# Weight rounding in blocks of 2048 columns and feed-forward rows rounded a whole tile at once, in a gated cross-attention kernel

## Chip, core and metric

The kernel runs on one core of a Trainium2 chip. The metric is the device time of one execution in microseconds (us). The engines named below are PE (TensorE), DVE (VectorE), ACT (ScalarE), POOL (GpSimd) and SP (SyncE, which here only issues DMAs). Each engine takes its instructions strictly in the order in which they stand in its queue, as the trace shows.

## What is computed

The reference updates 2048 rows of 512 numbers four times, each time as `x = x + tanh(gain) * layer(layernorm(x))`:

1. each row goes, by its token's class (one of four), through a gated linear unit whose three weights are one batch of the context (512x512);
2. a feed-forward layer with 2048 inner columns, in which activations and weights are rounded to a block float format;
3. an attention with eight heads;
4. a mixture of 64 experts and a shared one, six experts a row.

The change touches the second layer, and the first one in whose shadow the second one's weights are prepared. What the second computes is, shortened:

```python
def _quantize_mx(x, ebits, mfrac, emax_elem, max_norm):   # blocks of 32 along the last axis
    amax = max(abs(xb)); sexp = floor(log2(amax)) - emax_elem; scale = 2 ** sexp
    return _quantize_elem(xb / scale, ebits, mfrac, max_norm) * scale

def _mx_linear(x, w):
    return einsum('bsh,oh->bso', _q_act(x), _q_w(w))

gate = _mx_linear(x, w_gate)         # w_gate, w_up: 2048 x 512
up = _mx_linear(x, w_up)
inter = silu(gate) * up
return _mx_linear(inter, w_down)     # w_down: 512 x 2048
```

## The kernel before

Rows are worked in tiles of 128. There are three large stages in time: the first layer with the weights' rounding beside it, the feed-forward layer, and the attention together with the experts, which makes up more than half of the time and is not touched. In the first two stages the order on PE, ACT, DVE and POOL is written out by hand: the order of the calls in the program is the order in each engine's queue.

**The first stage** (lines 183 to 562). The 2048 rows are sorted by class into 19 tiles. The loop of lines 532 to 559 runs i from -2 to 18, each iteration working on neighbouring tiles: PE turns two tiles (`turned`, L459), turns a part of the rounded weights (`turn_weights`), multiplies by the context (`times_context`, L474, eight fp32 matmuls a call, two calls an iteration). ACT does the copies from PSUM, the silu (L481), the layernorm's application and sums, and DVE does one product a tile (`gated`, L486) and, every fourth tile, a chain of small instructions for the layernorm's factors (`row_factors`).

The rest of DVE's queue is filled with the rounding of the weights. `quantize` (L235) is a generator: it takes a block of 1024 columns by 128 partitions, and rounds it in ten DVE instructions and one ACT copy (L251, `mx_wide`, the block scales spread out to all columns). After each step it yields a number of microseconds, a guess of the step's time written in the code. `some_weights(us)` takes steps until their guesses have used up `us`. There are 24 blocks: 8 of each of the three weights. A rounded block goes to the list `rounded`; `turn_weights` takes one from it, and its eight PE transposes and two ACT copies bring it into `wgT`, `wuT` or `wdT` (L204, L205, L219, L221). What is left after the loop is done in lines 560 to 562. `fetch_weights` issues the DMA of a block on SP's queue: one block is fetched first of all, three after the context's second load.

**The feed-forward stage** (lines 565 to 747). For each of 16 tiles: `gate_up(j, c)` makes 512 gate columns and 512 up columns, each in a PSUM buffer of its own (`gu`, four buffers, four matmuls each, L642); `silu` (ACT, L652) reads the gate half; `times_up` (DVE, L656) multiplies by the up half and so frees that buffer. `block_scales` takes the maxima of blocks of 32 (L587), two small steps (L588, L590) and has ACT spread the scales (`mx_wide`, L592); `block_round` divides (L603), cuts off (L609) and multiplies by `mx_wide` (L610). `turned_hidden` and `turned_rows` transpose the rounded numbers on PE (L622) and copy them out on ACT (L623, into `iT` and `hT`); `down` makes the output (L662), `add_rows` scales it (L667) and adds it to the rows in memory with a DMA of POOL. The inner rows (2048 columns, called "a") are rounded in two halves of 1024 columns; the input rows (512 columns, called "h") are rounded one tile ahead. `load` (L578) reads a tile back from memory on SP's queue; the tiles of this stage lie in memory that the first stage has given up.

## Time and profile before

| | us |
|---|---|
| median of three runs (1250.85 to 1265.53) | 1256.01 |
| the profiled execution | 1259.73 |
| its span, first instruction to last | 1257.5 |

The profile comes from that one execution. The stages in it, with the busy time of three engines in us:

| stretch of the span, us | what | DVE | PE | ACT |
|---|---|---|---|---|
| 0 to 38.9 | sorting, context turned, first rows arrive | 23.32 | 13.60 | 12.70 |
| 38.9 to 62.2 | the first layer starts | 21.57 | 13.10 | 18.29 |
| 62.2 to 230.0 | its loop | 159.66 | 153.58 | 105.85 |
| 230.0 to 251.0 | the last tile and the last weights | 18.95 | 8.49 | 6.34 |
| 251.0 to 283.0 | the feed-forward starts | 15.75 | 9.00 | 18.71 |
| 283.0 to 491.3 | 14 tiles of it | 194.38 | 174.97 | 134.82 |
| 491.3 to 514.8 | its last two | 16.25 | 18.02 | 10.98 |
| 514.8 to 1257.5 | attention and experts | 349.07 | 627.66 | 257.74 |

Busy time leaves out the gaps of some tens of ns from one instruction to the next. In a timeline below, each line is: start in us, duration in us, engine, line of the code, operation, output tile and input tiles, shape, how many instructions were merged, and in brackets how long the engine had been idle before it and what ended that.

### The profile page before, as it was taken

The numbers are of one execution on the slowest core, as the hardware profiler recorded it, in microseconds if no ns is written. First come the engines' busy times: TensorE is split into PE (matmuls) and PEld (weight loads), VectorE is DVE, ScalarE is ACT, GpSimd is POOL, SyncE is SP. The second block draws the span as 40 slices with busy tenths as digits, with TensorE's granted clock in tenths as the row PEclk, the third lists the DMA queues.
The fourth block names the chain that finished last, engine by engine and source line by source line (L and its number), as shares of the span: only waits on it lengthen the run. The fifth ranks groups of instructions, "written<-read, shape, count | busy, mean of one in ns | idle before, by whom it ended". The sixth has DMA issues, their size and how long they took to land. (4 is left out here: it accounts for less than half of the span.)

```text
span 1257.5 us, 14877 instructions
## 1 busy us (share of the span) xinstructions
PE 1018.4 (81%) x4603; PEld 516.6 (41%) x4603; DVE 799.0 (64%) x1993; ACT 565.4 (45%) x1128; POOL 381.8 (30%) x526
## 2 busy tenths in 40 slices
PE   4489999528878788367999998982699999999994
PEld 4244454213434344133444444441355555544441
DVE  7799999949999999425888788774122222222221
ACT  3666765356767565245666666650111111211120
POOL 3023222100000000001354454455354444444424
PEclk9699999769999999687999999996799999999997
DMA  9834434221211111591112121119699999999977
GB/s 336 303 84 111 116 76 100 26 93 33 36 19 23 17 18 17 156 279 51 62 52 65 58 62 43 37 49 232 195 277 281 275 271 273 267 275 279 279 195 137
DMA packets 75806, 174.76 MB, mean 139 GB/s; under 512 B 13024, under 2 KB 14064, under 8 KB 75664
## 3 DMA queue, kind: packets, MB, share of 16 engines
q1 hardware_dynamic: 51696, 128.04, 34.3%
q0 software_dynamic: 23200, 45.16, 18.4%
q8 instruction: 38, 0.62, 0.2%
q10 hardware_dynamic: 832, 0.62, 0.2%
q14 instruction: 40, 0.33, 0.1%
HBM read 133.76 MB, written 44.20 MB: 142 GB/s over the span
## 5 line engine op out<-in xcount | busy, mean ns | idle before, releaser
L1188 PE MATMUL gu_ps<-e_gu,gT 128*96 128x384 f32 x512 | 178.1, 491 | 0.1
L1192 DVE SCALAR_TENSOR_TENSOR a<-s,xg,gu_ps 96x192 f32<-96x192 f32 x64 | 35.1, 548 | 153.4 <-ACT s L1190 153.4
L1211 PE MATMUL e_y<-e_dn,eaT 96*96 96x512 f32 x256 | 120.5, 592 | 0.1
L123 POOL DMA_INDIRECT taken<-token_no,to_i x96 | 97.1, 1011 | 48.8 <-issue 24.1
L848 ACT ACTIVATE p<-at_s,low 128x512 f32<-128x512 f32 x128 | 87.5, 695 | 50.5 <-DVE low L839 50.5
L834 PE MATMUL at_s<-c_tile,q 64*128 64x512 f32 x256 | 76.6, 679 | 37.1 <-ACT p L848 21.7
L1188 PEld LDWEIGHTS gu_ps<-e_gu,gT 128*96 128x96 f32 x512 | 79.2, 165 | 62.5 <-issue 62.2
L839 DVE TENSOR_REDUCE low<-at_s 128x2 f32<-128x1024 f32 x64 | 77.8, 1217 | 36.7 <-PE at_s L834 36.3
L1213 ACT COPY e_o<-e_y 96x512 f32<-96x512 f32 x64 | 37.3, 582 | 132.9 <-PE e_y L1211 61.3
L1180 DVE COPY gT<-g_ps 128x384 f32<-128x384 f32 x64 | 35.7, 558 | 94.4 <-PE g_ps L1178 94.4
L668 POOL DMA_DIRECT2D x_rows<-y_sb x16 | 13.7, 857 | 259.7 <-ACT y_sb L667 204.9
L859 ACT COPY pT<-p_ps 128x512 f32<-128x512 f32 x128 | 70.9, 597 | 41.3 <-PE p_ps L858 41.0
L491 POOL DMA_INDIRECT x_rows<-y_sb,to_row x19 | 37.1, 1955 | 152.9 <-ACT y_sb L490 152.9
L1214 POOL DMA_INDIRECT out_dram<-e_o,idx x34 | 48.8, 1435 | 114.4 <-ACT e_o L1213 52.7
L858 PEld LDWEIGHTS p_ps<-ident,p 128*128 128x128 f32 x512 | 56.7, 144 | 59.5 <-issue 24.2
L858 PE MATMUL p_ps<-ident,p 128*128 128x128 f32 x512 | 75.2, 287 | 6.6 <-ACT hT L936 6.4
L1165 POOL DMA_INDIRECT xg<-h_rows,idx x64 | 60.1, 938 | 64.4 <-DVE a L1192 29.2
L642 PEld LDWEIGHTS <-hT 128*128 128x128 bf16 x512 | 49.9, 101 | 70.0 <-issue 12.8
L474 PE MATMUL l_mm<-cT,sT 128*128 x152 | 75.9, 646 | 0.3 <-ACT sT L461 0.3
L642 PE MATMUL gu<-wgT,hT 128*128 128x512 bf16 x256 | 70.8, 402 | 6.4 <-ACT hT L623 6.4
L1190 ACT ACTIVATE s<-gu_ps 96x192 f32<-96x192 f32 x64 | 20.9, 327 | 119.1 <-PE gu_ps L1188 119.1
L474 PE MATMUL l_mm<-cT,hT 128*128 x152 | 71.5, 614 | 1.7 <-ACT hT L461 1.7
(239 smaller groups left out, 2019.7 us busy)
## 6 DMA issues: line engine op xcount, KB each, us to landing
e_gu<-in_L_ffn_w_gate_dram SPq DMA_DIRECT2D x64, 384.0 KB, 15.7
e_gu<-in_L_ffn_w_up_dram SPq DMA_DIRECT2D x64, 384.0 KB, 16.1
e_dn<-in_L_ffn_w_down_dram SPq DMA_DIRECT2D x64, 384.0 KB, 15.6
w_src<-in_L_ffn_w_gate_dram SPq DMA_DIRECT2D x8, 512.0 KB, 5.2
c_sb<-in_ctx_dram SPq DMA_DIRECT2D x4, 1024.0 KB, 8.3
w_src<-in_L_ffn_w_up_dram SPq DMA_DIRECT2D x8, 512.0 KB, 4.9
more_rows<-zeros SPq DMA_DIRECT2D x16, 256.0 KB, 8.1
w_src<-in_L_ffn_w_down_dram SPq DMA_DIRECT2D x8, 512.0 KB, 4.5
```

The lines of the kernel that those rows point to most:

```text
L123: ins = nc.gpsimd.indirect_dma_start(out=table[:, :], out_offset=bass.IndirectOffsetOnAxis(ap=to, axis=0), in_=what, in_offset=None)
L474: nc.tensor.matmul(ps.unsqueeze(1), aT[:, k, :], cT[:, bass.ds(at + k, 1), :], start=k == 0, stop=k == KC - 1)
L642: nc.tensor.matmul(ps, hT[:, k, :], wT[:, k, bass.ts(c, 512)], start=k == 0, stop=k == KC - 1)
L834: nc.tensor.matmul(s[:, h, :], t["q"][rows, bass.ts(i, P)], t["c"][rows, :], start=True, stop=True)
L839: nc.vector.tensor_reduce(low, tiles[j]["s", i], AX.X, ALU.max, negate=True)
L848: nc.scalar.activation(p[:, h, :], s[:, h, :], AF.Exp, bias=low[:, h : h + 1], accum_out=t["sums"][:, i, h : h + 1])
L858: nc.tensor.transpose(ps[:, k, :], p[:, h, bass.ts(k, P)], ident)
L859: nc.scalar.copy(tiles[j]["pT"][h][:, :, bass.ts(i, P)], ps)
L1165: nc.gpsimd.indirect_dma_start(out=g[:, :], out_offset=None, in_=h_rows[:, :], in_offset=bass.IndirectOffsetOnAxis(ap=idx[:, e : e + 1], a ...
L1188: nc.tensor.matmul(ps, gT[:, k, :], gu[:, :, k, :], start=k == 0, stop=k == KC - 1)
L1211: nc.tensor.matmul(y, aT[:, c, :], dn[:, c, :], start=c == 0, stop=c == 1)
L1214: nc.gpsimd.indirect_dma_start(out=tables[e % 2 if e < E - LAST else 0][:, :], out_offset=bass.IndirectOffsetOnAxis(ap=idx[:, e : e + 1], ...
```

## The change

The weights are rounded in 12 blocks of 2048 columns. The buffers of the sources go from 4 of 1024 columns to 3 of 2048, those of `w_q` from 3 to 2, those of `mx_wide` from 2 to 1; one block is fetched first and two more later. A rounded block is turned in two parts, each of eight transposes and now one ACT copy of 1024 columns. The guesses that `quantize` yields are new, and `some_weights` now carries over to its next call what a step took too much or too little. After the loop two parts are turned each time round.

In the feed-forward stage the inner rows are multiplied, rounded and turned a whole tile of 2048 columns at once; the order of the loop is new, and the input rows are rounded two tiles ahead.

```diff
-            src = qp.tile([P, 2, D], F32, name="w_src", bufs=4)
+            src = qp.tile([P, 4, D], F32, name="w_src", bufs=3)
...
-            def turn(q):
+            def turn(q, part):
...
-                    nc.scalar.copy(wT[:, k : k + 2, bass.ts(rb, 2 * P)], ps.rearrange("p i j q -> p i (j q)"))
+                nc.scalar.copy(wT[:, k : k + 2, bass.ts(rb, 4 * P)], ps.rearrange("p i j q -> p i (j q)"))
...
         def quantize():
-            n = 2 * D
+            n = 4 * D
...
-                yield 1.21
+                yield 2.3
...
-                wide = qp.tile([P, n], BF16, name="mx_wide")
+                wide = qp.tile([P, n], BF16, name="mx_wide", bufs=1)
...
-                rounded.append((turn, q))
-                yield 0.69
+                rounded.extend([(turn, q, 0), (turn, q, 1)])
+                yield 1.25
...
+        credit, ended = [0.0], []
         def some_weights(us):
-            while us > 0:
+            credit[0] += us
+            while credit[0] > 0:
                 took = next(weights, None)
...
-                us -= took
+                credit[0] -= took
...
                 if b == 1:
-                    fetch_weights(3)
+                    fetch_weights(2)
...
-        while rounded or sources:
-            some_weights(8.0)
+        while rounded or not ended:
+            some_weights(16.0)
+            turn_weights()
             turn_weights()
...
+        times_up(0, 0)
+        gate_up(0, 2)
+        silu(0, 2)
+        times_up(0, 1)
+        gate_up(0, 3)
+        silu(0, 3)
         for j in range(4, 6):
             sums_of(j)
+        block_scales(1, "h", D)
+        block_round(1, "h", D)
+        turned_rows(1)
```

The guesses of the nine steps go from 1.21, 0.36, 1.22, 0.69, 0.69, 1.22, 1.22, 0.5, 0.69 to 2.3, 0.4, 2.3, 1.25, 1.25, 2.3, 2.3, 0.7, 1.25. The loop over the tiles of the feed-forward, before and after:

```python
# before
if j:
    turned_hidden(j - 1, 1)
times_up(j, 0)
times_up(j, 1)
gate_up(j, 2)
silu(j, 2)
block_scales(j, ("a", 0), half_n)
block_round(j, ("a", 0), half_n)
gate_up(j, 3)
silu(j, 3)
if j:
    down(j - 1)
if j + 8 < NT:
    load(j + 8)
sums_of(j + 6)
if j + 2 < NT:
    normal(j + 2)
if more:
    block_scales(j + 1, "h", D)
    block_round(j + 1, "h", D)
if j:
    add_rows(j - 1)
if more:
    turned_rows(j + 1)
turned_hidden(j, 0)
if more:
    gate_up(j + 1, 0)
    silu(j + 1, 0)
times_up(j, 2)
times_up(j, 3)
block_scales(j, ("a", 1), half_n)
if more:
    gate_up(j + 1, 1)
    silu(j + 1, 1)
block_round(j, ("a", 1), half_n)
factors_from(j + 3)
```

```python
# after
times_up(j, 2)
times_up(j, 3)
block_scales(j, "a", FI)
if more:
    gate_up(j + 1, 0)
    silu(j + 1, 0)
    gate_up(j + 1, 1)
    silu(j + 1, 1)
if j:
    down(j - 1)
block_round(j, "a", FI)
if j + 8 < NT:
    load(j + 8)
if j + 2 < NT:
    normal(j + 2)
sums_of(j + 6)
if j:
    add_rows(j - 1)
if more:
    times_up(j + 1, 0)
    times_up(j + 1, 1)
    gate_up(j + 1, 2)
    silu(j + 1, 2)
    gate_up(j + 1, 3)
    silu(j + 1, 3)
turned_hidden(j)
if j + 2 < NT:
    block_scales(j + 2, "h", D)
    block_round(j + 2, "h", D)
    turned_rows(j + 2)
factors_from(j + 3)
```

`turned_hidden(j)` now makes 16 transposes into two PSUM buffers and two ACT copies of 1024 columns into `iT`.

More of the change, by code (lines that the diff above doesn't have):

```diff
@@ L193, in rows_of @@
         def rows_of(w, wT, rb):
-            src = qp.tile([P, 2, D], F32, name="w_src", bufs=4)
-            nc.sync.dma_start(src, w[bass.ts(rb, 2 * P), :].rearrange("(j p) d -> p j d", p=P))
-            def turn(q):
-                q = q.rearrange("p (j d) -> p j d", j=2)
-                for k in range(0, KC, 2):
-                    ps = ps_t.tile([P, 2, 2, P], BF16, name="w_ps", tag="t")
-                    for i in range(2):
-                        for j in range(2):
-                            nc.tensor.transpose(ps[:, i, j, :], q[:, j, bass.ts(k + i, P)], ident_bf)
-                    nc.scalar.copy(wT[:, k : k + 2, bass.ts(rb, 2 * P)], ps.rearrange("p i j q -> p i (j q)"))
@@ L207, in rows_of @@
-            return src.rearrange("p j d -> p (j d)"), turn
-        def half_row_of_down(ob, half):
-            n = FI // 2
-            src = qp.tile([P, n], F32, name="w_src", bufs=4)
-            nc.sync.dma_start(src, w_down[bass.ts(ob, P), bass.ts(half, n)])
-            def turn(q):
-                for c in range(0, n // P, 4):
-                    ps = ps_t.tile([P, 4, P], BF16, name="w_ps", tag="t")
-                    for i in range(4):
-                        nc.tensor.transpose(ps[:, i, :], q[:, bass.ts(c + i, P)], ident_bf)
-                    at = half * (n // P) + c
-                    nc.scalar.copy(wdT[:, at : at + 4, bass.ts(ob, P)], ps)
+            src = qp.tile([P, 4, D], F32, name="w_src", bufs=3)
@@ new lines, in rows_of @@
+            nc.sync.dma_start(src, w[bass.ts(rb, 4 * P), :].rearrange("(j p) d -> p j d", p=P))
+            def turn(q, part):
+                q = q.rearrange("p (j d) -> p j d", j=4)
+                ps = ps_t.tile([P, 2, 4, P], BF16, name="w_ps", tag="t")
+                k = 2 * part
+                for i in range(2):
+                    for j in range(4):
+                        nc.tensor.transpose(ps[:, i, j, :], q[:, j, bass.ts(k + i, P)], ident_bf)
+                nc.scalar.copy(wT[:, k : k + 2, bass.ts(rb, 4 * P)], ps.rearrange("p i j q -> p i (j q)"))
@@ new lines, in rows_of, with row_of_down, turn @@
+            return src.rearrange("p j d -> p (j d)"), turn
+        def row_of_down(ob):
+            src = qp.tile([P, FI], F32, name="w_src", bufs=3)
+            nc.sync.dma_start(src, w_down[bass.ts(ob, P), :])
+            def turn(q, part):
+                ps = ps_t.tile([P, 8, P], BF16, name="w_ps", tag="t")
+                for i in range(8):
+                    nc.tensor.transpose(ps[:, i, :], q[:, bass.ts(8 * part + i, P)], ident_bf)
+                nc.scalar.copy(wdT[:, bass.ts(part, 8), bass.ts(ob, P)], ps)
@@ L223, in half_row_of_down @@
             return src, turn
-        blocks = [(rows_of, (w, wT, rb)) for rb in range(FI // (2 * P)) for w, wT in ((w_gate, wgT), (w_up, wuT))]
-        blocks += [(half_row_of_down, (ob, half)) for ob in range(KC) for half in range(2)]
+        blocks = [(rows_of, (w, wT, rb)) for rb in range(FI // (4 * P)) for w, wT in ((w_gate, wgT), (w_up, wuT))]
+        blocks += [(row_of_down, (ob,)) for ob in range(KC)]
         sources, rounded = deque(), deque()
@@ L249, in quantize @@
                 nc.vector.tensor_scalar(inv.bitcast(I32), top.bitcast(I32), -1.0, float(254 << 23), ALU.mult, ALU.add)
-                wide = qp.tile([P, n], BF16, name="mx_wide")
+                wide = qp.tile([P, n], BF16, name="mx_wide", bufs=1)
                 nc.scalar.copy(wide.rearrange("p (k b) -> p k b", b=BLK), top.unsqueeze(2).to_broadcast([P, nb, BLK]))
-                yield 0.36
+                yield 0.4
                 nc.vector.tensor_tensor(s3, s3, inv.unsqueeze(2).to_broadcast([P, nb, BLK]), ALU.mult)
-                yield 1.22
+                yield 2.3
                 e = qp.tile([P, n], F32, name="mx_e", bufs=1)
                 nc.vector.tensor_scalar(e.bitcast(I32), src.bitcast(I32), EXP_MASK, None, ALU.bitwise_and)
-                yield 0.69
+                yield 1.25
                 nc.vector.tensor_scalar(e, e, 0.25, None, ALU.max)
-                yield 0.69
+                yield 1.25
                 nc.vector.scalar_tensor_tensor(src, e, magic, src, ALU.mult, ALU.add)
-                yield 1.22
-                q = qp.tile([P, n], BF16, name="w_q", bufs=3)
+                yield 2.3
+                q = qp.tile([P, n], BF16, name="w_q")
                 nc.vector.scalar_tensor_tensor(q, e, -magic, src, ALU.mult, ALU.add)
                 fetch_weights(1)
-                yield 1.22
+                yield 2.3
                 nc.vector.tensor_scalar(q, q, 1.5, -1.5, ALU.min, ALU.max)
-                yield 0.5
+                yield 0.7
                 nc.vector.tensor_mul(q, q, wide)
-                rounded.append((turn, q))
-                yield 0.69
+                rounded.extend([(turn, q, 0), (turn, q, 1)])
+                yield 1.25
         left = deque(blocks)
         weights = quantize()
+        credit, ended = [0.0], []
         def some_weights(us):
-            while us > 0:
+            credit[0] += us
+            while credit[0] > 0:
                 took = next(weights, None)
                 if took is None:
+                    ended.append(True)
                     return
-                us -= took
+                credit[0] -= took
         def turn_weights():
             if rounded:
-                turn, q = rounded.popleft()
-                turn(q)
+                turn, q, part = rounded.popleft()
+                turn(q, part)
         def turn_context(b):
@@ L628, in turned_rows, with turned_hidden @@
             stages[j]["hT"] = hT
-        def turned_hidden(j, half):
-            if half == 0:
-                stages[j]["iT"] = fp.tile([P, FI // P, P], BF16, name="iT")
-            n = FI // 2
-            turned(j, ("a", half), n, ps_a, stages[j]["iT"], half * (n // P))
+        def turned_hidden(j):
+            iT = fp.tile([P, FI // P, P], BF16, name="iT")
+            q = stages[j].pop(("q", "a"))
+            n = FI // P // 2
+            for half in range(2):
+                ps = ps_a.tile([P, n, P], BF16, name="q_ps", tag="q_ps")
+                for c in range(n):
+                    nc.tensor.transpose(ps[:, c, :], q[:, bass.ts(half * n + c, P)], ident_bf)
+                nc.scalar.copy(iT[:, bass.ts(half, n), :], ps)
+            stages[j]["iT"] = iT
         def gate_up(j, c):
@@ L646, in silu @@
         def silu(j, c):
-            half = c // 2
-            if c % 2 == 0:
-                stages[j]["a", half] = fp.tile([P, FI // 2], F32, name="inter")
-            part = stages[j]["a", half][:, bass.ts(c % 2, 512)]
+            if c == 0:
+                stages[j]["a"] = fp.tile([P, FI], F32, name="inter")
+            part = stages[j]["a"][:, bass.ts(c, 512)]
             nc.scalar.activation(part, stages[j]["gu", c][0], AF.Silu, scale=16.0)
         def times_up(j, c):
-            part = stages[j]["a", c // 2][:, bass.ts(c % 2, 512)]
+            part = stages[j]["a"][:, bass.ts(c, 512)]
             nc.vector.tensor_mul(part, part, stages[j].pop(("gu", c))[1])
@@ L685, in factors_from @@
                     stages[t]["stats"] = s
-        half_n = FI // 2
         for j in range(8):
@@ L703, in flamingo_kernel @@
         silu(0, 1)
+        times_up(0, 0)
[4 more added lines that the diff above has]
+        silu(0, 3)
         for j in range(4, 6):
             sums_of(j)
+        block_scales(1, "h", D)
+        block_round(1, "h", D)
+        turned_rows(1)
         for j in range(NT):
+            times_up(j, 2)
+            times_up(j, 3)
+            block_scales(j, "a", FI)
             more = j + 1 < NT
-            if j:
-                turned_hidden(j - 1, 1)
-            times_up(j, 0)
-            times_up(j, 1)
-            gate_up(j, 2)
-            silu(j, 2)
-            block_scales(j, ("a", 0), half_n)
-            block_round(j, ("a", 0), half_n)
-            gate_up(j, 3)
-            silu(j, 3)
+            if more:
+                gate_up(j + 1, 0)
+                silu(j + 1, 0)
+                gate_up(j + 1, 1)
+                silu(j + 1, 1)
             if j:
                 down(j - 1)
+            block_round(j, "a", FI)
             if j + 8 < NT:
                 load(j + 8)
-            sums_of(j + 6)
             if j + 2 < NT:
                 normal(j + 2)
-            if more:
-                block_scales(j + 1, "h", D)
-                block_round(j + 1, "h", D)
+            sums_of(j + 6)
             if j:
@@ L731, in flamingo_kernel @@
             if more:
-                turned_rows(j + 1)
-            turned_hidden(j, 0)
-            if more:
-                gate_up(j + 1, 0)
-                silu(j + 1, 0)
-            times_up(j, 2)
-            times_up(j, 3)
-            block_scales(j, ("a", 1), half_n)
-            if more:
-                gate_up(j + 1, 1)
-                silu(j + 1, 1)
-            block_round(j, ("a", 1), half_n)
+                times_up(j + 1, 0)
[5 more added lines that the diff above has]
+            turned_hidden(j)
+            if j + 2 < NT:
+                block_scales(j + 2, "h", D)
+                block_round(j + 2, "h", D)
+                turned_rows(j + 2)
             factors_from(j + 3)
-        turned_hidden(NT - 1, 1)
         down(NT - 1)
```

## The prediction, made before the changed kernel ran

> **What bounds the kernel now.** I read the page's forty slices first, then busy time by stage, then the timelines of DVE, ACT and PE over two tiles of the feed-forward, then those of the first stage and SP's waits.

> ```profile
> DVE  7799999949999999425888788774122222222221
> ```

> Slices are 31.4 us. DVE is full in slices 3 to 7 (the first layer with the weights' rounding) and 9 to 15 (the feed-forward). These are the two stretches that the change touches. DVE's timeline around one half of the inner rows:

> ```profile
> 400.50 0.68 DVE L587 TENSOR_REDUCE mx_top<-h 128x16 f32<-128x512 f32 x1
> ...
> 402.36 0.43 DVE L609 TENSOR_SCALAR mx_c<-mx_q 128x512 bf16<-128x512 fp8e4 x1
> 402.89 0.43 DVE L610 TENSOR_TENSOR mx_c<-mx_c,mx_wide 128x512 bf16<-128x512 bf16 x1
> 403.23 1.28 DVE L656 TENSOR_TENSOR inter<-inter,gu 128x512 f32<-128x512 f32 x2
> 404.55 1.22 DVE L587 TENSOR_REDUCE mx_top<-inter 128x32 f32<-128x1024 f32 x1
> ...
> 406.24 1.23 DVE L603 TENSOR_TENSOR mx_q<-inter,mx_inv 128x1024 fp8e4<-128x1024 f32 x1
> 407.49 0.69 DVE L609 TENSOR_SCALAR mx_c<-mx_q 128x1024 bf16<-128x1024 fp8e4 x1
> 408.29 0.69 DVE L610 TENSOR_TENSOR mx_c<-mx_c,mx_wide 128x1024 bf16<-128x1024 bf16 x1
> 408.90 1.28 DVE L656 TENSOR_TENSOR inter<-inter,gu 128x512 f32<-128x512 f32 x2
> ```

> No line has an idle bracket: a half takes 408.90 - 403.23 = 5.67, the input rows 403.23 - 400.50 = 2.73, a tile 2 x 5.67 + 2.73 = 14.07. The reduction costs 0.71 start to start at 512 columns and 1.25 at 1024, so some 0.17 of each instruction is fixed. ACT and PE in the same tile:

> ```profile
> 401.42 0.62 ACT L592 CAST mx_wide<-mx_top 128x512 bf16<-128x512 f32 x1
> ...
> 403.81 0.59 ACT L623 COPY hT<-q_ps 128x512 bf16<-128x512 bf16 x1 [0.58 <-PE q_ps L622]
> 404.29 1.02 ACT L623 COPY iT<-q_ps 128x1024 bf16<-128x1024 bf16 x1
> ```

> The scales of the input rows are spread (401.42) before any `iT` copy: the copy stands early in ACT's queue, and DVE finds it done. That is what the change turns round.

> ```profile
> SPq L578 <- DMA x_rows<-y_sb,to_row: 29.8, 1, 29.8
> SPq L578 <- DVE w_q L268: 3.4, 1, 3.4
> SPq L578 <- PE w_ps L219: 1.1, 1, 1.1
> ```

> SP's waits show what the feed-forward's first load (issued at 251.07) waited for in turn: the first layer's last rows in memory, then the last block's rounding, last its transposes.

> **First stage, change by change.** Prices of 2048 columns are extended from the rows of 512 and 1024. A block of 1024 takes 8.06 (from 233.68 to 241.74). At 2048: reduction 2.33, two small steps 0.5, division 2.29, mask and maximum 1.27 each, the two roundings 2.33 each, cut 0.80, product 1.15: 14.27. In all 24 x 8.06 = 193.4 becomes 12 x 14.27 = 171.2.

> Where that falls follows from the guesses. Before, each of the 21 iterations gets exactly one block (4.17 and 3.63 of guesses), two go ahead of the loop, one is left. After, the guesses sum to 12 x 14.05 = 168.6, and the calls hand out 14.5 + 42 x 3.6 = 165.7: only the last cut and product are left. From the first rows' arrival (38.9) to the last `gated` (ends 230.0) DVE's weight steps are 161.8 before and 147.0 after. I take 14 off, since the trace runs 1 under its own rows here.

> Behind that last `gated`, the load comes at +21.0. After, 11.9 of DVE steps remain, then 16 transposes, eight in 0.83 at the slow pace of 508.44: 13.6, so -7.

> Against it: PE needs 8.25 a tile in unbroken stretches (87.83 to 96.08), 18 tiles 148.5, while DVE's own sum for these falls to 9.3 blocks (132.7), 18 products (10.8) and four chains of factors (13.2): 156.7. Eight us of play over 18 tiles is little, and from iteration 9 the copy L251 falls in the second call of its iteration, where ACT, waiting for a reduction of 2.3, holds up the copy of `sT` queued behind it, and PE's product with it. Between 0 and +8, I take +4, the middle: no row shows it. And 3 MB of weights instead of 2 go ahead of the first rows' gathers in a stretch where the DMA is 91% busy at 313 GB/s: 0 to +3.3, I take +2, as half of the megabyte stands ahead of the context. Sum: -14 - 7 + 4 + 2 = **-15** (-22 to -9). The two-part turns with one copy of 1.01 for two that take 1.07 cost nothing: ACT has 105.9 of 167.8 busy in that loop.

> **Feed-forward, DVE alone.** A block of 2048: reduction 2.33, small steps 0.5, division 2.29, cut 1.34, product 1.15, together 7.61; with four L656 (2.64) 10.25 instead of 11.34. DVE alone would need 10.25 + 2.73 = 12.98 a tile, 1.09 less.

> **Feed-forward, the new wait.** The last instruction of the input rows (L610) needs `mx_wide`, and in the new order ACT's copy for it is queued behind both `iT` copies of the tile. Put tile j's L656 for column 2 at 0. The block ends at 8.93, the next tile's L656 for column 0 at 9.61, for column 1 at 10.25, and DVE reaches the input rows' L610 at 12.64. On the other side: of the four `gu` buffers, that L656 frees the one that `gate_up(j+1, 2)` wants for its up half. PE goes on 0.06 later (as at 427.00), does three groups of four at 0.866 (up 2, gate 3, up 3): 12.27. Then `turned_hidden`: its first copy starts 0.66 after the transposes (409.04 to 409.70): 12.93; the two copies take 0.91 each start to start: 14.75; then `mx_wide` 0.60: 15.35. So L610 runs at 15.38, **2.74 late**, and the next tile starts at 15.72. Queued behind L610 on DVE is the next tile's L656, and PE's `turned_rows` waits for it. ACT is no bound on the way: its spread of 2048 (about 1.9, from 0.62 and 1.04) is done at 5.9, y at 10.0.

> PE restarts at 1.22 (L610 to the first gate matmul was 1.56) and has, up to gate 2, five groups and 16 matmuls of `down` (3.47): it ends at 9.02, 0.65 before its wait. But it has been idle for 2.5 us and done 0.25 of transposes. What such a gap does:

> ```profile
> 77.90 0.92 PE L204 MATMUL w_ps<-ident_bf,w_q 128*128 128x128 bf16 x8 [2.57 <-DVE w_q L268]
> 78.61 5.08 PE L474 MATMUL l_mm<-cT,sT 128*128 x8
> 83.52 3.60 PE L474 MATMUL l_mm<-cT,hT 128*128 x8
> ...
> 115.90 1.04 PE L204 MATMUL w_ps<-ident_bf,w_q 128*128 128x128 bf16 x8 [2.53 <-DVE w_q L268]
> 116.72 4.80 PE L474 MATMUL l_mm<-cT,sT 128*128 x8
> ```

> The eight matmuls behind the gap take 1.2 to 1.5 longer than the eight after them; at 153.76 and 191.18 gaps of 2.50 do the same. In the feed-forward, restarts cost 0.93 (284.37 to 288.76 for four groups, 3.46 when undisturbed) to 1.69 (435.87 to 441.02). Less the 0.65 of play: 0.3 to 1.0 a tile, so 16.0 to 16.8; I take 16.4. [...]

> Sum over 14 tiles, from L656 of column 2 in tile 0 to the same in tile 14: before 491.30 - 282.95 = 208.3. After, eleven at 16.4, three at 15.7 behind which DVE's factors (3.3, as at 422.97) give PE the time to recover, and those factors: 180.4 + 47.2 + 9.9 = 237.5, **+29.2** (all warm 230.0, +21.7; all at 16.8 241.9, +33.6). Start: `mx_wide` of tile 1 follows silu 3 and four sums on ACT, so that L656 starts at 282.4 instead of 282.95, -0.5. End: the last tile's L656 of column 3 waits for PE until 12.5, its block ends at 20.8, and the last output copy comes 5.76 later as before plus a second `iT` copy of 0.91: 27.5 instead of 514.06 - 491.30 = 22.8, +4.7 (4.2 to 5.2). Feed-forward **+33.4** (25.4 to 38.3). `load`, `normal` and the sums move by a few us inside the tile and hold up nobody: the rows are loaded eight tiles ahead. The later stages (742.7) are unchanged.

> **Sum.** +33.4 - 15 = +18.4. The profiled execution (1259.7, span 1257.5) would become 1278; it lies 3.7 over the median, and on the median it is 1256.0 + 18.4 = 1274, 1259 to 1285 with all bounds.

> **Rivals.** *The wait doesn't come (faster).* If `mx_wide` were done when DVE reaches L610, each tile takes 12.98: 14 x 12.98 + 9.9 - 208.3 = -16.7, with ends -12.5, with the first stage -27.5: 1228. It hangs on one number, the 2.74: below 1.96 the change breaks even, below 1.06 it is faster by over 1%. For it: `h` itself is ready early. Against: ACT ran in program order wherever I looked, and the 2.74 doesn't contain any extended price of DVE; it is PE's and ACT's steps behind one L656 (5.8) less 3.0 of DVE. *PE stays warm:* +25.9 - 15 = +10.9, 1267. *The first stage doesn't pay:* PE's 8.25 and ACT's held copies eat 10 of the 14, so -5: 1284.

> **Chances.** Forecast 0.50, warm 0.20, first stage unpaid 0.14, no wait 0.16. One per cent, about what can be told from no change, is 12.6 us: 1243.4 to 1268.6. Slower: most of the forecast, all of the unpaid first stage: 0.58. Same: most of the warm case and the forecast's low end: 0.27. Faster: 0.15. The range leaves out the case without the wait and little else: 1250 to 1290.

> **What would show it.** L610 of the input rows idle for 2.7 to 3.5 before it, ended by ACT `mx_wide`; tiles of 16 to 17; PE's four-groups above 1.03 behind each such gap; the first load at 233 to 240. Wrong would be: DVE without idle time in the feed-forward, or a first load later than 245.

## The result, and the profile after

| | before | after |
|---|---|---|
| median, four runs each | 1255.89 | 1302.11 (1299.60 to 1303.33) |
| profiled execution / its span | 1259.73 / 1257.5 | 1302.19 / 1300.4 |
| first load of the feed-forward issued | 251.07 | 263.45 |
| from there to the last `y_sb` | 262.99 | 294.97 |
| from there to the end | 743.4 | 742.0 |

The ratio is 1.036 (1.029 to 1.042): slower, and above the range of 1250 to 1290. The feed-forward lost 32.0 (forecast 33.4). The first stage was to gain 15 and lost 12.4; nearly the whole miss is there. Line numbers of the changed kernel are a few higher: `gated` is L487, `turned` L460 and L462, `times_context` L475, the rounding's last step L612, `times_up` L663.

The forty slices of the changed kernel, DVE's row, now 32.5 us each:

```profile
DVE  7788778737877787731688888786222222222231
```

Neither stretch that was full of 9s before is full now: DVE waits in both. Its timeline over one tile of the feed-forward:

```profile
413.91 1.28 DVE L663 TENSOR_TENSOR inter<-inter,gu 128x512 f32<-128x512 f32 x2
415.23 2.29 DVE L589 TENSOR_REDUCE mx_top<-inter 128x64 f32<-128x2048 f32 x1
...
425.85 0.43 DVE L611 TENSOR_SCALAR mx_c<-mx_q 128x512 bf16<-128x512 fp8e4 x1
430.31 0.43 DVE L612 TENSOR_TENSOR mx_c<-mx_c,mx_wide 128x512 bf16<-128x512 bf16 x1 [4.03 <-ACT mx_wide L594]
430.65 1.28 DVE L663 TENSOR_TENSOR inter<-inter,gu 128x512 f32<-128x512 f32 x2
```

A tile takes 430.65 - 413.91 = 16.74, of which 4.03 is the wait for `mx_wide`; the reduction of 2048 columns takes 2.29, as it was extended (2.33). ACT's timeline in the same tile shows what `mx_wide` is queued behind:

```profile
427.83 1.93 ACT L641 COPY iT<-q_ps 128x1024 bf16<-128x1024 bf16 x2 [0.71 <-PE q_ps L640]
429.64 0.63 ACT L594 CAST mx_wide<-mx_top 128x512 bf16<-128x512 f32 x1
```

And PE's timeline shows what the wait does to its clock (four matmuls take 1.03 when undisturbed):

```profile
430.79 0.40 PE L624 MATMUL q_ps<-ident_bf,mx_c 128*128 128x128 bf16 x4 [2.55 <-DVE mx_c L612]
431.86 1.44 PE L650 MATMUL gu<-wgT,hT 128*128 128x512 bf16 x4 [0.68 <-ACT hT L625]
433.10 1.91 PE L650 MATMUL gu<-wuT,hT 128*128 128x512 bf16 x4
434.81 1.51 PE L650 MATMUL gu<-wgT,hT 128*128 128x512 bf16 x4
436.15 1.03 PE L650 MATMUL gu<-wuT,hT 128*128 128x512 bf16 x4
```

The granted clock of the profile is 0.50 of full speed from 432.35 to 435.76, and 1.00 before and after.

A wait, a gap and slow groups of this kind the prediction had described. What it hadn't is in the first stage. There, DVE's product `gated` (L486 before, now L487) had no idle time ahead of it before (0.0); now it has 25.3 in all, 25.1 of it ended by ACT's silu (L482). In these two lines, the first from before, stand the busy time of all 19, the mean ns of one, and the idle time ahead of them:

```profile
L486 DVE TENSOR_TENSOR s<-s,l_mm 128x512 f32<-128x512 f32 x19 | 12.9, 680 | 0.0
```

```profile
L487 DVE TENSOR_TENSOR s<-s,l_mm 128x512 f32<-128x512 f32 x19 | 13.0, 685 | 25.3 <-ACT s L482 25.1
```

One such wait, followed back through three timelines of the changed kernel: DVE, ACT, PE.

```profile
93.62 2.29 DVE L260 SCALAR_TENSOR_TENSOR w_q<-mx_e,w_src 128x2048 bf16<-128x2048 f32 x1
99.24 0.69 DVE L487 TENSOR_TENSOR s<-s,l_mm 128x512 f32<-128x512 f32 x1 [3.33 <-ACT s L482]
```

```profile
93.91 1.01 ACT L205 COPY wgT<-w_ps 128x1024 bf16<-128x1024 bf16 x1 [3.99 <-PE w_ps L204]
94.81 0.81 ACT L170 ACTIVATE h<-xs,ln_shift,ln_y 128x512 f32<-128x512 f32 x1
...
97.66 0.56 ACT L462 COPY sT<-l_ps 128x512 f32<-128x512 f32 x1
...
98.60 0.61 ACT L482 ACTIVATE s<-l_mm 128x512 f32<-128x512 f32 x1
```

```profile
93.26 0.61 PE L204 MATMUL w_ps<-ident_bf,w_q 128*128 128x128 bf16 x8
...
95.68 0.66 PE L460 MATMUL l_ps<-ident,h 128*128 128x128 f32 x4 [1.37 <-ACT h L170]
98.28 5.17 PE L475 MATMUL l_mm<-cT,sT 128*128 x8 [1.94 <-ACT sT L462]
103.28 3.60 PE L475 MATMUL l_mm<-cT,hT 128*128 x8
```

Read from the bottom. The loop has a second `turn_weights` for the case that more than one part waits in `rounded`; it stands behind both products of the iteration. Before, one block of one part came each iteration, and it ran once, in the first iteration, since two blocks were ready ahead of the loop (PE's eight transposes at 52.65, behind a product). Now a block adds two parts in every second iteration, and it runs each time:

```python
            if waiting > 1:
                turn_weights()
            if i + 3 < NS:
                normal(i + 3)
```

Its eight transposes (93.26) come only when PE is through its products, so ACT stood idle for 3.99 before the copy of the turned part (93.91), although the factors that the `normal` behind it reads had been ready since 68.4. Behind this copy were queued `normal` (94.81), the output rows, the sums, and then `sT` (97.66). PE waited 1.37 and 1.94 for these, its next eight matmuls took 5.17 instead of 3.65 after the gap, and the silu and DVE's product came late. Such a pair of iterations takes 20 to 23 us (from the transposes of L460 at 85.01 to 106.71, 126.95, 149.86), against 2 x 9.3 before. The DVE work did fall as computed (the weights' steps are busy 167.1 in all, 187.1 before), and DVE waited instead.

SP's waits of the changed kernel, for the feed-forward's first load, have one line left of the three:

```profile
SPq L580 <- DMA x_rows<-y_sb,to_row: 60.1, 1, 60.1
```

PE's last transposes of weights end at 259.0; the load, issued at 263.45, waits last for the last tile's rows, whose `y_sb` is at 257.39.

### The profile page after: what moved, and what is told of

Read it like the earlier page. It is cut to its first block, busy times and chain, and to the rows that moved or that the text cites. A ratio compares the mean times of both kernels' runs of the same rounds, so it can differ in the third digit from the quotient of the medians.

```text
span 1300.4 us, 14538 instructions
## 1 busy us (share of the span) xinstructions
PE 1036.2 (80%) x4603; PEld 521.6 (40%) x4603; DVE 765.3 (59%) x1777; ACT 558.6 (43%) x1076; POOL 386.6 (30%) x526
## 4 chain that ended last, share of the span: by engine, by line
PE 41%; DMA 14%; DVE 11%; ACT 7%; issue 3%; POOL 1%; SPq 0%; DVEq 0%; POOLq 0%; ACTq 0%
PE gu L650 9%; DMA out_dram<-e_o,idx 8%; PE gu_ps L1197 8%; PE e_y L1220 5%; PE first_ps L952 3%; PE y L669 3%; PE at_o L900 3%; DVE low L848 3%; PE at_s L843 2%; PE sh_y L1274 2%; ACT iT L641 2%; PE p_ps L867 2%; ACT p L857 1%; DMA e_gu<-in_L_ffn_w_gate_dram 1%; DMA e_dn<-in_L_ffn_w_down_dram 1%
## 5 line engine op out<-in xcount | busy, mean ns | idle before, releaser
L857 ACT ACTIVATE p<-at_s,low 128x512 f32<-128x512 f32 x128 | 87.5, 695 | 53.8 <-DVE low L848 51.9
L475 PE MATMUL l_mm<-cT,sT 128*128 x152 | 83.5, 700 | 16.4 <-ACT sT L462 16.4
L650 PE MATMUL gu<-wgT,hT 128*128 128x512 bf16 x256 | 77.2, 431 | 21.9 <-ACT hT L625 13.9
L650 PEld LDWEIGHTS <-hT 128*128 128x128 bf16 x512 | 53.9, 108 | 98.8 <-issue 38.5
L650 PE MATMUL gu<-wuT,hT 128*128 128x512 bf16 x256 | 75.8, 425 | 0.0
```

Of the source, the lines that this page charges most:

```text
L475: nc.tensor.matmul(ps.unsqueeze(1), aT[:, k, :], cT[:, bass.ds(at + k, 1), :], start=k == 0, stop=k == KC - 1)
L650: nc.tensor.matmul(ps, hT[:, k, :], wT[:, k, bass.ts(c, 512)], start=k == 0, stop=k == KC - 1)
L857: nc.scalar.activation(p[:, h, :], s[:, h, :], AF.Exp, bias=low[:, h : h + 1], accum_out=t["sums"][:, i, h : h + 1])
```

## The experiments

Theory: the first stage's loss is the second turn's ACT copy, queued behind PE's products and ahead of ACT's work for the next tile; the feed-forward's loss is `mx_wide` behind the `iT` copies, and the clock that PE loses in the gap. Rivals: the first stage loses through the DMA of larger blocks or through PE's load, or PE's place for the transposes is at fault rather than ACT's; in the feed-forward, two copies ahead of `mx_wide` aren't enough, or the clock has nothing to do with it. All eight kernels ran in two groups; the kernel before had a median of 1250.51 beside the first (the two halves, the early second turn, the input rows first) and of 1259.10 beside the second. So ratios are compared, and the stages of the profiles:

| | ratio to before | first load | to last `y_sb` | rest | L487 / L612 wait |
|---|---|---|---|---|---|
| before | 1 | 251.07 | 262.99 | 743.4 | 0.0 / 3.4 |
| after | 1.036 | 263.45 | 294.97 | 742.0 | 25.3 / 54.3 |
| feed-forward alone | 1.0296 | 251.55 | 295.22 | 742.5 | 0.8 / 54.0 |
| weights alone | 1.0147 | 259.55 | 265.10 | 735.0 | 22.4 / 3.2 |
| second turn ahead of the products | 1.0166 | 231.80 | 295.54 | 742.1 | 3.3 / 54.5 |
| second turn's copy behind the sums | 1.0101 | 233.69 | 294.74 | 740.9 | 2.5 / 53.8 |
| input rows ahead of turned inner rows | 0.9997 | 264.20 | 249.63 | 733.4 | 26.2 / 8.5 |
| only their scales ahead | 1.0043 | 260.10 | 257.52 | 744.9 | 22.6 / 13.2 |
| spare transposes in the gap | 1.0193 | 262.80 | 279.28 | 739.2 | 24.8 / 38.3 |
| both orders mended | 0.9742 | 232.49 | 249.45 | 741.9 | 3.4 / 7.2 |

"First load" is when the feed-forward's first load is issued; the L612 column is what DVE waits there for ACT's `mx_wide`. The rest, which no kernel touches, lies between 733.4 and 744.9: hence the stages, not the totals, carry the readings.

**The two halves of the change.** The first kernel has the feed-forward of the change behind the first stage of before, the second the first stage of the change ahead of the feed-forward of before.

> First stage of before, feed-forward of the change. In the changed kernel the feed-forward, from its first load to its last output copy, takes 295.0 us (263.45 to 558.42) against 263.0 before (251.07 to 514.06), and the first load comes 12.4 later. If the two halves of the change add up: first load at 251, feed-forward 295, time 1256 + 32 = 1288. Rival, that the feed-forward is slow because of what the first stage leaves behind (the layout of the memory, a colder PE): well under 1288, near 1256.

> First stage of the change, feed-forward of before. If the halves add up: first load at 263.5, feed-forward 263.0, time 1256 + 12.4 = 1268. Rival as in the run beside it: 1256 or 1300.

Measured: 1288.23, ratio 1.0296 (1.0250 to 1.0341), and 1265.85, 1.0147 (1.0112 to 1.0181). In the profiles the feed-forward costs 32.2 with the old first stage too, and the first stage 8.5 with the old feed-forward, with 22.4 of L487's waits. So each half loses without the other. Whether the first stage's loss is the same in both (8.5 here, 12.4 in the whole change) can't be told: in the five kernels with this first stage the first load lies between 259.55 and 264.20. That 1288 was met is in part luck: the first kernel took 37.7 longer than the kernel before in its own group, and 32.7 longer by the stages.

**The second turn directly behind the first, ahead of both products.** The work is the same; only the place in the queues of PE and ACT changes.

```diff
             if waiting:
                 turn_weights()
+            if waiting > 1:
+                turn_weights()
...
-            if waiting > 1:
-                turn_weights()
             if i + 3 < NS:
```

> The second part's turn moves up behind the first one's, ahead of both products. Theory: the 27 us between the forecast for the first stage (first load 15 earlier) and what came (12.4 later) are ACT's queue, held by the second part's copy until PE has done two products. Then the first load comes at 236 to 243, DVE's waits for the silu go from 24 us to under 8, and the time is 1275 to 1282. Rival, that blocks of 2048 are at fault themselves (steps of 2.3 us, an ACT spread of 1.9, later fetches): first load within 4 of 263, time within 5 of 1302.

Measured: 1270.59, ratio 1.0166 (1.0143 to 1.0190). The first load comes at 231.80, 31.7 before the changed kernel's and 19.3 before the old one's; load and time both come below what was expected. In PE's timeline of this kernel the 16 transposes stand together, and the products follow each other:

```profile
80.36 1.06 PE L204 MATMUL w_ps<-ident_bf,w_q 128*128 128x128 bf16 x16
81.26 3.65 PE L475 MATMUL l_mm<-cT,sT 128*128 x8
...
89.45 3.70 PE L475 MATMUL l_mm<-cT,sT 128*128 x8 [0.24 <-ACT sT L462]
```

On ACT the two copies run as soon as `sT` and `hT` are out, with no idle time in front:

```profile
81.09 1.95 ACT L205 COPY wgT<-w_ps 128x1024 bf16<-128x1024 bf16 x2
```

The larger blocks, their DMA and all transposes are still in this kernel: they are not what the first stage lost by.

**PE's place or ACT's.** The second turn stays behind both products on PE; its transposes come as late as in the changed kernel. On ACT its copy moves behind `normal`, the output rows and the sums.

```diff
-            if waiting > 1:
-                turn_weights()
             if i + 3 < NS:
                 normal(i + 3)
...
             sums_of(i + 7)
+            if waiting > 1:
+                turn_weights()
```

> The second part's turn stays behind both products on PE, but moves on ACT behind the layernorm's application, the output copy and the sums. PE's own order is as in the changed kernel. Theory: it is ACT's order that costs, so nearly all of the first stage's loss comes back: first load at 231 to 238, time 1270 to 1278. Rival, that it is the place of the transposes on PE: first load at 263, time 1302.

Measured: 1273.44, ratio 1.0101 (1.0057 to 1.0145), first load at 233.69. ACT's timeline of this kernel:

```profile
142.12 1.01 ACT L205 COPY wuT<-w_ps 128x1024 bf16<-128x1024 bf16 x1 [1.15 <-PE w_ps L204]
143.03 0.59 ACT L462 COPY sT<-l_ps 128x512 f32<-128x512 f32 x1
```

ACT still waits for the transposes, but 1.15 instead of 3.99, because the work that was queued behind the copy is now done while PE multiplies. PE's wait for `sT` is 11.0 in all, against 16.4 in the changed kernel and 7.3 with the early turn. 29.8 of the 31.7 us come from ACT's order alone.

**The input rows ahead of the turned inner rows.** In the feed-forward's loop, the three calls for the input rows move ahead of `turned_hidden(j)`, so ACT spreads their scales before it copies `iT`.

```diff
-            turned_hidden(j)
             if j + 2 < NT:
                 block_scales(j + 2, "h", D)
                 block_round(j + 2, "h", D)
                 turned_rows(j + 2)
+            turned_hidden(j)
```

> In the feed-forward, scales, rounding and turn of the input rows go ahead of the turn of the inner rows; the first stage is the change's. Theory: without ACT's copies ahead of the spread scales, DVE never waits and a tile takes 12.98; 14 tiles take 191.6 with the factors instead of 235.0, so the time is 1302 - 43 = 1259, the feed-forward 252. Rival, that rounding a whole tile of 2048 at once makes the chain too long wherever the scales stand: tiles stay above 15, time above 1290.

Measured: 1249.73, ratio 0.9997 (0.9969 to 1.0024), with the first stage's loss still in it. DVE's timeline of this kernel over a tile:

```profile
413.83 1.28 DVE L663 TENSOR_TENSOR inter<-inter,gu 128x512 f32<-128x512 f32 x2
...
417.42 0.42 DVE L612 TENSOR_TENSOR mx_c<-mx_c,mx_wide 128x512 bf16<-128x512 bf16 x1
...
426.65 1.28 DVE L663 TENSOR_TENSOR inter<-inter,gu 128x512 f32<-128x512 f32 x2
```

The tile takes 12.82 and L612 doesn't wait; the prediction had 12.98 for DVE alone. The feed-forward takes 249.63, 13.4 less than before the change (the prediction's rival without the wait had 12.5) and 45.3 less than after it; against the first stage's loss of 13.1 in this profile that makes the ratio of 1. So the blocks of 2048 columns do pay what DVE's prices say, if the order lets them.

**Only the scales ahead.** Here `mx_wide` is ahead of `iT` on ACT, but the rounded input rows are still turned behind the inner rows on PE, and `hT` copied behind `iT`.

```diff
+            if j + 2 < NT:
+                block_scales(j + 2, "h", D)
             turned_hidden(j)
             if j + 2 < NT:
-                block_scales(j + 2, "h", D)
```

> In the feed-forward only the scales of the input rows (and with them ACT's spread) go ahead of the turn of the inner rows; their rounding's turn, and the copy of hT, stay behind it. Theory: DVE's wait for the spread goes, since it hung on that one copy's place; what is left is the loop of PE and ACT, from the first gate matmul over twelve groups, down, 16 transposes, two copies and the copy of hT back to it, 13.5 a tile against DVE's 12.8: time some 10 above the 1250 of the run with the whole turn moved, 1255 to 1265. Rival, that the turn and the copy of hT behind the inner rows were the harm and not the spread: tiles above 15, time above 1285.

Measured: 1262.27, ratio 1.0043 (1.0012 to 1.0075); the feed-forward takes 257.52. DVE's wait falls to 0.78 in a tile (13.2 in all), but now PE waits for `hT`, as its timeline shows:

```profile
432.99 0.81 PE L650 MATMUL gu<-wgT,hT 128*128 128x512 bf16 x3 [2.00 <-ACT hT L625]
433.64 1.03 PE L650 MATMUL gu<-wuT,hT 128*128 128x512 bf16 x4
```

Of the 45.3 us that the full order gains, the place of `mx_wide` alone gives 37.5; the other 7.9 is `hT` behind `iT`. Note that the groups after this gap of 2.00 are at full pace. But in the same kernel the shorter gaps of 1.42 and 0.90 around the four transposes at 446.71 are followed by groups of 1.87 and 1.91.

**Spare transposes in PE's gap.** The order of the change is kept, with its wait for `mx_wide`. Ahead of each `turned_rows` PE does 40 transposes of the unit matrix, whose result the real ones overwrite.

```diff
+            for c in range(spare):
+                nc.tensor.transpose(ps[:, c % 4, :], ident_bf, ident_bf)
...
-            turned(j, "h", D, ps_h, hT, 0)
+            turned(j, "h", D, ps_h, hT, 0, spare=40 if j > 1 else 0)
```

> The changed kernel with 40 idle transposes of the unit matrix ahead of each turn of the input rows, into the buffer that the turn then overwrites, so that PE is not idle while it waits. Theory: the tiles that take 16.7 do so since PE's clock falls in the gap of 2.5 us and the next groups of four take 1.4 to 1.9 instead of 1.03; kept busy, these tiles take 15.7 as forecast without the clock, the wait of DVE goes from 4.0 to 2.8, 11 tiles x 1.0 = 11 off, 1291. Rival, that the gap has nothing to do with the slow groups: no change, 1302, groups still slow.

Measured: 1283.97, ratio 1.0193 (1.0156 to 1.0229). PE's timeline of this kernel:

```profile
434.35 2.40 PE L624 MATMUL q_ps<-ident_bf 128*128 128x128 bf16 x40
437.06 0.40 PE L626 MATMUL q_ps<-ident_bf,mx_c 128*128 128x128 bf16 x4 [0.32 <-DVE mx_c L612]
438.37 0.81 PE L652 MATMUL gu<-wgT,hT 128*128 128x512 bf16 x3 [0.91 <-ACT hT L627]
439.01 1.03 PE L652 MATMUL gu<-wuT,hT 128*128 128x512 bf16 x4
```

And DVE's:

```profile
421.87 1.28 DVE L665 TENSOR_TENSOR inter<-inter,gu 128x512 f32<-128x512 f32 x2
...
436.58 0.43 DVE L612 TENSOR_TENSOR mx_c<-mx_c,mx_wide 128x512 bf16<-128x512 bf16 x1 [2.34 <-ACT mx_wide L594]
436.92 1.28 DVE L665 TENSOR_TENSOR inter<-inter,gu 128x512 f32<-128x512 f32 x2
```

The order of the calls and the wait for `mx_wide` are those of the change; PE only isn't idle meanwhile. The groups stay at 1.03, the wait at L612 falls from 4.03 to 2.34 a tile, the tile to 15.05 and the feed-forward from 294.97 to 279.28, more than expected. The granted clock over the 14 tiles is 0.99 here (295.62 to 514.64) and 0.92 in the changed kernel (294.97 to 529.99); over the whole execution it is 0.924 and 0.912. The rival that the slow groups have nothing to do with the gap falls. So 15.7 of the feed-forward's 32.0 were the clock, about half. The other 16.3 are what the order costs at a full clock, less what the larger blocks gain: against the 249.63 of the kernel with the input rows first, the order alone costs 29.7.

**Both orders mended.** The early second turn and the input rows first, together.

> The second part's turn ahead of both products, and the input rows ahead of the inner ones. Of the changed kernel's 1302, the first edit alone took 31 off and the second 52, in stages that follow one another. If they add up: 1302 - 31 - 52 = 1219, first load at 232, feed-forward 244 to 251, 2 to 3% faster than before. Rival, that what one gains the other gives back (the first load waits for something else once the feed-forward is quick, the later stages start with less fetched): 1230 or more.

Measured: 1227.21, ratio 0.9742 (0.9707 to 0.9777), faster than the kernel before by 2.6%. Both stages keep what they had alone: the first load comes at 232.49, 18.6 earlier, and the feed-forward takes 249.45, 13.5 less. 1259.10 less these is 1227.0. The time lies between the expected 1219 and the rival's 1230; the expectation is too low because it was reckoned from the lower times of the first group, and the stages speak against the rival.

## Why the prediction was wrong

**The step that failed** is the last sentence on the first stage: "The two-part turns with one copy of 1.01 for two that take 1.07 cost nothing: ACT has 105.9 of 167.8 busy in that loop." It compared busy times and never asked where the second part's copy stands in ACT's queue, and what releases it. It stands behind both of PE's products and ahead of `normal`, the output rows, the sums and the next `sT`. By the moved turn this placement, put at nothing, cost 31.7 us, by the moved copy alone 29.8. Up to 12 of these can be the clock in PE's gaps: the products with `sT` are busy 83.5 in all in the changed kernel and 71.4 with the early turn. A share of busy time says that an engine could do the work; it says nothing on when, if one instruction at the head of the queue waits for another engine. That the branch for a second waiting part was there, ran once before and would run in every second iteration, could be read from the code. The prediction's own sign of being wrong, a first load later than 245, came: 263.45.

**The other terms of the first stage** held, as the kernel with the early turn shows: it gains 19.3 (forecast 15, bounds 9 to 22). Its last `gated` ends at 217.3 instead of 230.1, 12.9 earlier: -14 of DVE's work, with little left of the +4 for ACT and PE and of the +2 for early DMA (in the changed kernel the first sums start at 38.05 instead of 37.20, +0.85). The held copy of `mx_wide` for which the +4 stood comes in this kernel too: ACT waits for its reductions four times, 8.0 in all, `sT` comes behind it, and PE waits 2.85 for `sT` at 152.47. Its tail is 14.5 instead of 21.0: -6.5, forecast -7. In the changed kernel the last `gated` ends at 245.9, 15.8 later instead of 8 earlier, and the tail is 17.5. The miss of 24 up to there answers to L487's 25.3 of waits.

**The rival "the first stage doesn't pay"** named the right suspects, PE's 8.25 and ACT's held copies, but priced them at 10, with `mx_wide` of the weights as the held copy instead of the turned parts, and so its 1284 fell short too.

**The feed-forward** was right in mechanism and nearly in size: +32.0 for +33.4; the 14 tiles take 235.0 (294.97 to 529.99) for 237.5, the end 28.4 for 27.5. The wait ahead of L612 is 3.4 in the mean (54.3 over 16), as 2.7 to 3.5 was written; a tile that follows a slowed PE has 4.03, and at a full clock it is 2.34, where the sum had 2.74. The tile shown takes 16.74 for the 16.4 taken, the one ahead of it, behind a chain of factors, 14.8 for 15.7. "PE stays warm" was not this kernel; where the spare transposes make it so, the feed-forward is 16.3 longer than before, and that rival had 25.9, with tiles of 15.72 for the 15.05 measured. So two misses offset each other: 9.6 too much for the wait at a full clock, and 8.2 too little for the clock (7.5 for 15.7). That the sum came within 1.4 is in part luck.

**The clock rule.** In the changed kernel, idle gaps of 2.55 and 0.68 around 0.40 of transposes were followed by groups of up to 1.91 in most tiles. The prediction's rule, that each such gap costs, is too simple: three of the eleven tiles have the gap and no slow group.

## What to carry to other kernels

For each instruction whose number or place changes, ask which engine releases it and what is queued behind it on its own engine; an engine that is 63% busy (ACT's 105.9 of 167.8 before the change) can still hold up all the others by standing at a copy whose input comes last (ACT stood 3.99 at one such copy). Look for branches that hardly ever ran and that a new size will take (here `waiting > 1`). And when a change of size makes a kernel slower, try the order of the calls before the size is given up: a few moved lines turned +3.6% into -2.6%.

## What the runs showed of the hardware

The same gap doesn't always slow PE. In the changed kernel's feed-forward, each of the eleven tiles whose transposes of the input rows start from 309.82 to 481.50 has the same 2.55 and 0.68 of idle time ahead of its first group, but the first two groups behind it take 1.04 and 1.03 in the tiles at 327.63, 395.94 and 464.26, and up to 1.91 in others; these three are 68.3 us apart. In the first stage the gap of 1.37 and 1.94 is followed by eight matmuls in 5.17 at 98.28 and 163.13, in 3.70 at 119.98 and 184.88, and in 6.38 at 140.21: each pair is 64.9 apart. So the length of the gap alone doesn't decide. In the feed-forward four tiles of the program make 68.3 too, so that this repetition by itself shows little.

```profile
428.94:432.35 3.41, 0.88 (x7) 0.48 (x8) 2.01 (x4) 1.92 (x3) 0.00 (x0) 1.00 0.00 0
432.35:435.76 3.41, 3.41 (x10) 1.18 (x9) 3.31 (x4) 1.25 (x1) 0.00 (x0) 0.50 0.00 0
435.76:439.18 3.42, 3.42 (x18) 1.52 (x17) 3.28 (x3) 3.39 (x7) 0.00 (x0) 1.00 0.00 0
459.66:463.07 3.41, 2.05 (x22) 1.29 (x20) 0.09 (x1) 2.37 (x3) 0.00 (x0) 1.00 0.63 77
463.07:466.48 3.41, 1.54 (x10) 0.79 (x11) 2.31 (x13) 1.26 (x3) 0.00 (x0) 1.00 0.00 0
466.48:469.90 3.42, 2.51 (x13) 1.04 (x12) 3.30 (x9) 0.00 (x0) 0.00 (x0) 1.00 0.00 0
```

In the first tile the gap leaves PE 0.88 of busy time in one step, and the next step has half the clock. In the second the same gap falls across two steps, PE is busy for 2.05 and 1.54 of them, and the clock stays full. From 295 to 540 in this kernel, each step at full clock with less than 1.4 of busy PE is followed by one at half clock, and each with more than 1.5 by one at full clock. In its first stage the border is less sharp: 1.7 was followed once by half the clock (70.54) and once by the full one (241.20). So in this trace the fall of the clock goes with how much of a gap falls into one step of the grid.

The distances of 68.3 and 64.9 are 20.0 and 19.0 steps of this grid, so that equal gaps that far apart fall on it alike. No run here shifted a gap against the grid on purpose; the reading rests on where the gaps happen to fall in these traces.
